# A planned issue order with new durations, due times and join rounds: an audio tower on one core

## The chip, the cores and the metric

The kernel runs on 1 core of one Trainium2 chip. The time is the device time of one execution in microseconds (us). Three runs before the change took 18586.4, 18587.15 and 18591.35 us; their median is 18587.15.

## What is computed

A batch of 32 signals is cut into S = 313 frames of 512 samples. A DCT, one attention layer and one feed-forward layer follow:

```python
h = einsum('bfh,kh->bfk', frames, D)                     # DCT
h = h + attention(layernorm(h))
h = h + ffn(layernorm(h))

# attention, 8 heads of 64
Q, K = xpos(X W_Q), xpos(X W_K); V = X W_V
p = softmax(Q K^T) * gamma^|i-j|
Y = groupnorm(p V)
return (silu(X W_G) * Y) W_O

# ffn: 256 units n, over 512 features d
theta = x[d] / (1 + |W[n,d]|) + B[n,d]
idx = round(theta * 4096/2pi) mod 4096
cos_sum[n] = sum_d cos(idx) * attn_cos[n,d]              # the same with sin
return silu(cos_sum proj_cos^T + sin_sum proj_sin^T)
```

Nearly all the work is in the feed-forward layer: 32 x 313 x 256 x 512 angles, each with a sine and a cosine.

## The kernel before, in words

**Feed-forward in rounds.** The 256 units are taken in 8 blocks of 32 (UNITS), and the sequences in pairs. A round (ffn_round, line 574) does one block for all pairs that are in the ring; a pair is in the ring for 8 rounds in a row, one for each block. STARTS (line 33) names the round in which each of the 16 pairs joins. A ring of one to four pairs means r = 2, 4, 6 or 8 sequences side by side. A slot holds 24 sequence-columns of S: 12 units of 2 sequences, 6 of 4, 4 of 6 or 3 of 8. For each slot VectorE (DVE) writes the indices as int16, one instruction per unit (line 612), adds a quarter turn for the cosine in a second tile (621), and masks both (628). ScalarE (ACT) makes two sine tiles of 128 x 7512 elements from them (line 636). TensorE (PE) sums each tile over features with one-hot weights, 24 products a tile (line 658), into PSUM banks pa; at the end of a round VectorE copies the sums out (675) and SP stores them. There are five index tiles (N_IX) and two sine tiles (N_TRIG): ACT cannot start the second tile after one that TensorE still reads. SP loads the block's one-hot weights (604), the factors f (592) and the normalised inputs xT (596).

**Attention in between.** Each sequence has to have gone through DCT, layer norm, attention and the second layer norm before its pair can join. The function attention (line 302) does this for one sequence in the buffers of A. Its stages: the product with the DCT by rows (line 282), a layer norm on VectorE (245 to 260) whose reciprocal root is a Newton iteration of 12 small steps on GpSimd (POOL, lines 233 to 236), transposes (269), values by rows, four times queries and keys by columns (297) with a rotary step on VectorE, scores (374) with maximum and subtraction on VectorE (382, 385), exponentials on ACT (400, or 404 where few pairs run), per head transposes (428), decay (440) and value products (446), the gate by columns, group norm with a second Newton chain (three columns times eight heads), output product by rows, second layer norm, and a store of xT to memory. The first two sequences run before the first sine, in two sets of buffers A and B. Output (line 528) multiplies a pair's finished sums by the projection and adds the residual.

**What sets the order.** Nothing is scheduled at run time: each engine runs its instructions in a fixed order. The class Plan collects operations with a key (when it is due), an engine, a duration in ns and what it reads and writes. Its emit walks through them with one clock for each engine: on the engine that is free first it issues, among what is ready by then, the operation with the lowest key. A result on another engine counts as ready 300 ns later (WAIT), a DMA 2500 ns after its issue (LAND). One unit of key is one full sine tile; key_of[rd] is the number of such tiles before round rd. The feed-forward's operations have the key of their tile. Attention of a sequence has a window of keys (times, lines 797 to 804, spread so that each pair is finished 8 tiles before it joins), and its stages' keys are spread over that window by step (line 309):

```python
def step(n=1.0):
    done[0] += n
    return keys(done[0] / 135.0)
```

where the stages together add up to 139. The durations are the third argument of plan.add, as 880 for a row product (line 281), 550 for a column product (296), 800 for three transposes (273, 432), 660 for scores (373), 1000 for three value products (452), 6000 for a Newton chain (239), 150 for each product of the sums (666).

Of the kernel before, what the change touches and what calls it, by code (L numbers as in the profile page):

```python
# [22 lines left out]
HOP = 512  # L23
# [2 lines left out]
LUT = 4096  # L26
NC4 = HOP // P
EPS = 1e-5
RING = 8
UNITS = 32  # L30
SLOT = 24

STARTS = (0, 4, 8, 10, 12, 14, 16, 18, 20, 22, 24, 26, 28, 30, 32, 34)
NT = 3


# [6 lines left out]
DMA_NS = 500.0  # L43
# [83 lines left out]
def tile_audio_tower(ctx: ExitStack, tc: tile.TileContext, t: dict, out: bass.AP):  # L127
    nc = tc.nc
    n_seq, S = t["frames"].shape[0], t["frames"].shape[3]
    STEP = (S - 1) // NT  # L130
    N = S - STEP * (NT - 1)
# [89 lines left out]
    def rsqrt(plan, key, val, r, u, kv, kr, ku):  # L221

        def seed():
            nc.vector.tensor_scalar(
                u.bitcast(I32), val.bitcast(I32), 1, None, ALU.logical_shift_right
            )
            nc.vector.tensor_scalar(  # L227
                r.bitcast(I32), u.bitcast(I32), -1.0, float(RSQRT_SEED), ALU.mult, ALU.add
            )

        def newton():
            for _ in range(3):
                nc.gpsimd.tensor_tensor(u, r, r, ALU.mult)  # L233
                nc.gpsimd.tensor_tensor(u, u, val, ALU.mult)
                nc.gpsimd.tensor_scalar(u, u, -0.5, 1.5, ALU.mult, ALU.add)
                nc.gpsimd.tensor_tensor(r, r, u, ALU.mult)

        plan.add(key, "DVE", 400, seed, (kv,), (kr, ku))
        plan.add(key, "POOL", 6000, newton, (kv,), (kr, ku))

    def layernorm(plan, key, x):

# [21 lines left out]
    def transposed(plan, key, x):  # L264

        for c in range(NC4):
            def go(c=c):
                for i in range(NT):
                    nc.tensor.transpose(
                        x.W[:, c, ROW0[i] : ROW0[i] + N], x.h[:N, i, c * P : (c + 1) * P],  # L270
                        ident[:N, :N],
                    )
            plan.add(key, "PE", 800, go, x.rows_of, x.banks(c))

    def rows(plan, key, x, lhsT, src, r, order=range(NT), src_r=()):

        for c in range(NC4):
            k = x.load(plan, key, src[c], src_r)
            for to, i in enumerate(order):
                plan.add(  # L280
                    key, "PE", 880,
                    lambda c=c, i=i, k=k, to=to: nc.tensor.matmul(  # L282
                        x.W[:N, to, :], lhsT[:, c, ROW0[i] : ROW0[i] + N], x.ring[k],
                        start=(c == 0), stop=(c == NC4 - 1)
                    ),
                    (*r, x.k("ring", k)), x.banks(to),
                )

    def columns(plan, key, x, bank, src):

        k = x.load(plan, key, src)

        w = x.ring[k].rearrange("p (c n) -> p c n", n=P)
        for c in range(NC4):
            plan.add(
                key, "PE", 550,
                lambda c=c: nc.tensor.matmul(x.W[:, bank, :S], w[:, c, :], x.xnT[:, c, :],  # L297
                                             start=(c == 0), stop=(c == NC4 - 1)),
                (x.k("xnT"), x.k("ring", k)), x.banks(bank),
            )  # L300

    def attention(plan, keys, sq, x, eng, swap_m=None):
# [3 lines left out]

        done = [0.0]

        def step(n=1.0):
            done[0] += n  # L310
            return keys(done[0] / 135.0)

        def residual(key, load):
            for i in range(NT):
# [5 lines left out]
                else:  # L320
# [2 lines left out]

        hs, probs, room, us = x.rows_of, x.probs, x.room, x.every("u", 2)
        W3 = x.W[:N, :NT, :]
        plan.add(step(0), "SP", DMA_NS, lambda: nc.sync.dma_start(x.u, t["frames"][sq]), (), us)
        rows(plan, step(7), x, x.u, t["dct"], us)
        copy(plan, step(), eng, NT * HOP, x.h[:N], W3, x.banks(0, 1, 2), hs)
        residual(step(0), False)
        layernorm(plan, step(3), x)  # L330
        transposed(plan, step(3), x)
        copy(plan, step(), eng, NC4 * S, x.xnT, x.W[:, :, :S], x.banks(0, 1, 2, 3), (x.k("xnT"),))


        rows(plan, step(7), x, x.xnT, wv_d, (x.k("xnT"),), range(NT - 1, -1, -1),
             ("wv_d",))
        copy(plan, step(), eng, NT * HOP, x.h[:N], W3, x.banks(0, 1, 2), hs)
        plan.add(step(0), "POOL", 500, lambda: nc.gpsimd.memset(x.h[0:1, : NT - 1, :], 0.0), (), hs)

        plan.add(step(0), "SP", DMA_NS, lambda: nc.sync.dma_start(x.table, t["turn_qk"]),  # L340
                 (), probs[-4:-2])

        def rotary(g):
            key = step(4)
            qk, kq = x.qk[g % 2], x.k("u", g % 2)
            columns(plan, key, x, 0, t["wq"][g])
            columns(plan, key, x, 1, t["wk"][g])

            if swap_m is None:
                columns(plan, key, x, 2, t["wq_s"][g])  # L350
                columns(plan, key, x, 3, t["wk_s"][g])
            else:
                copy(plan, key, eng, 2 * S, x.raw, x.W[:, 0:2, :S], x.banks(0, 1), probs[-1:])
                for i in range(2):
                    plan.add(key, "PE", 550,
                             lambda i=i: nc.tensor.matmul(x.W[:, 2 + i, :S], swap_m, x.raw[:, i, :],
                                                          start=True, stop=True),
                             probs[-1:], x.banks(2 + i))
            plan.add(key, "DVE", 1500,
                     lambda: nc.vector.tensor_tensor(x.turn, x.W[:, :, :S], x.table, ALU.mult),  # L360
                     (*probs[-4:-2], *x.banks(0, 1, 2, 3)), probs[-2:])
            plan.add(key, "DVE", 870,
                     lambda: nc.vector.tensor_tensor(
                         qk, x.turn[:, 0:2], x.turn[:, 2:4], ALU.add),
                     probs[-2:], (kq,))

        def scores(hd):
            key = step(2.5)
            r0 = (hd % 2) * DH
            qk, kq = x.qk[hd // 2 % 2], x.k("u", hd // 2 % 2)  # L370
            for i in range(NT):
                plan.add(
                    key, "PE", 660,
                    lambda i=i: nc.tensor.matmul(  # L374
                        x.W[:N, i, :S], qk[r0 : r0 + DH, 0, ROW0[i] : ROW0[i] + N],
                        qk[r0 : r0 + DH, 1, :], start=True, stop=True,
                    ),
                    (kq,), x.banks(i),
                )
# [17 lines left out]
        def exps():  # L397
# [3 lines left out]
            else:  # L401
                for a in range(H):
# [2 lines left out]
                                             accum_out=x.sm[:N, i, a : a + 1])  # L405

            nc.scalar.activation(x.lu[:1, 0:1], x.lu[:1, 0:1], AF.Silu)
        plan.add(step(2), "ACT", 18200 if eng == "ACT" else 9500, exps,
                 (), [*probs, x.k("sm"), x.k("lu")])
        if eng == "DVE":  # L410
            for a in range(0, H, 2):
                plan.add(step(0), "DVE", 2080,
                         lambda a=a: nc.vector.tensor_reduce(
                             x.sm[:N, :, a : a + 2].rearrange("p i h -> p h i"),
                             x.prob[:N, a : a + 2], AX.X, ALU.add),
                         probs[a : a + 2], (x.k("sm"),))
        for hd in range(H):
            key = step(5)
            a, d = hd, hd % 2
            plan.add(key, "SP", DMA_NS,  # L420
                     lambda hd=hd, d=d: nc.sync.dma_start(x.dec[d], t["decay"][hd]),
# [1 line left out]
            for jj in range(NT):  # L423
                j = NT - 1 - jj

                def go(a=a, jj=jj, j=j):
                    for i in range(NT):
# [1 line left out]
                            x.W[:N, jj, ROW0[i] : ROW0[i] + N],  # L429
                            x.prob[:N, a, i, ROW0[j] : ROW0[j] + N], ident[:N, :N],  # L430
                        )
                plan.add(key, "PE", 800, go, (probs[a],), x.banks(jj))

            def decayed(a=a, d=d):
                window = x.dec[d][:N].rearrange("p (a s) -> p a s", a=1)
# [7 lines left out]
            for i in range(NT):  # L443
                def go(i=i, hd=hd, a=a):
                    for jj in range(NT):
# [3 lines left out]
                            x.h[:N, jj, hd * DH : (hd + 1) * DH],  # L449
                            start=(jj == 0), stop=(jj == NT - 1),  # L450
                        )
                plan.add(key, "PE", 1000, go, (probs[a], hs[hd // 2]), x.banks(3))
            if hd % 2 == 0:
                continue


            h0 = hd - 1
            plan.add(
                step(), "DVE", 560,
                lambda h0=h0: nc.vector.tensor_copy(  # L460
                    x.h[:N, :, h0 * DH : (h0 + 2) * DH], x.y[:N]),
                x.banks(3), (hs[h0 // 2],),
            )


        key = step(6)
        for g in range(NC4):
            columns(plan, key, x, g, t["wg"][g])
        plan.add(step(), "ACT", 1270,
                 lambda: nc.scalar.activation(x.u, x.W[:, :, :S], AF.Silu),  # L470
                 x.banks(0, 1, 2, 3), us)


        xh = x.h[:N].rearrange("p i (h e) -> p (i h) e", e=DH)
        key = step(5)
        if eng == "ACT":
            plan.add(key, "ACT", 1500,
                     lambda: nc.scalar.activation(x.sq[:N], x.h[:N], AF.Square), hs, room)
# [22 lines left out]
                 (x.k("gr"),), hs)  # L501


        transposed(plan, step(4), x)
        residual(step(0), True)
        key = step(2)
        for c in range(NC4):
            plan.add(key, "DVE", 530,
                     lambda c=c: nc.vector.tensor_scalar(
# [2 lines left out]
                     x.banks(c), room)  # L512
        plan.add(key, "DVE", 1460,
                 lambda: nc.vector.tensor_tensor(x.u, x.u, x.aff, ALU.mult), room, us)
        rows(plan, step(7), x, x.u, t["wo"], us)
        plan.add(step(2), "DVE", 1760,
                 lambda: nc.vector.tensor_tensor(x.h[:N], x.h[:N], W3, ALU.add),
                 x.banks(0, 1, 2), hs)
        residual(step(0), False)
        layernorm(plan, step(3), x)  # L520
        transposed(plan, step(3), x)
        key = step()
        copy(plan, key, eng, NC4 * S, x.u, x.W[:, :, :S], x.banks(0, 1, 2, 3), us)
        plan.add(key, "SP", DMA_NS,
                 lambda: nc.sync.dma_start(xT_d[:, :, sq * S : (sq + 1) * S], x.u),
# [48 lines left out]
    def ffn_round(plan, k0, blk, ring):  # L574
# [9 lines left out]
        key = k0  # L584
        for parts in slots:
# [45 lines left out]
            for k in (1, 0):  # L631
# [13 lines left out]
                def go(k=k, w=w, parts=parts, first=first):  # L645
# [4 lines left out]
                    for nc2 in dict.fromkeys((n // 2, c) for n, c in parts):  # L650
                        for bk, p in enumerate(banks[k]):
                            alone = r - 4 * bk == 2
                            for pt, (n, c) in enumerate(parts):
                                u = n % 2
                                for b in range(min(4, r - 4 * bk) if (n // 2, c) == nc2 else 0):
# [7 lines left out]
                                        stop=(n - u == UNITS - 2 and c == NC4 - 1  # L663
                                              and (alone or u == 1)),
                                    )
                plan.add(key, "PE", 150 * len(parts) * r, go,
                         (("trig", w), *(("hot", hot[n // 4 * 4, c]) for n, c in parts)),
                         [("pa", p) for p in banks[k]])
                key += len(parts) * r / SLOT
# [270 lines left out]
```

## Time and profile before

| what | us |
|---|---|
| median of three runs | 18587.15 |
| the profiled execution | 18593.15 |
| its span, first to last instruction | 18591.2 |
| ScalarE busy (of it sine tiles, line 636) | 17827.2 (17398.1) |
| VectorE busy (indices 6499.2, quarter turns 2905.2, masks 5581.8) | 17165.7 |
| TensorE busy (sums, line 658: 10304.5) | 14520.5 |
| GpSimd busy | 968.9 |

The mean granted clock of TensorE is 0.918 of full speed. A group's "busy" is the time in which at least one of its instructions ran; consecutive sines overlap a little at their ends, so that one lasts 6.45 us from its start to its end and 6.36 from one start to the next. "Idle before" names what ended a wait. The profile can be cut into stretches of time; since rounds are told by counting sine tiles in ACT's order, each round has a place in time: round 0 begins at 316 us, round 4 (the second pair joins) at 1017, round 14 (the sixth pair) at 4555, round 34 (the last pair) at 15777.

### The profile page before, as it was taken

The numbers are of one execution on the slowest core, as the hardware profiler recorded it, in microseconds if no ns is written. First come the engines' busy times: TensorE is split into PE (matmuls) and PEld (weight loads), VectorE is DVE, ScalarE is ACT, GpSimd is POOL, SyncE is SP. The second block draws the span as 40 slices with busy tenths as digits, with TensorE's granted clock in tenths as the row PEclk, the third lists the DMA queues.
The fourth block names the chain that finished last, engine by engine and source line by source line (L and its number), as shares of the span: only waits on it lengthen the run. The fifth ranks groups of instructions, "written<-read, shape, count | busy, mean of one in ns | idle before, by whom it ended". The sixth has DMA issues, their size and how long they took to land. (4 is left out here: it accounts for less than half of the span.)

```text
span 18591.2 us, 325962 instructions
## 1 busy us (share of the span) xinstructions
PE 14520.5 (78%) x148768; PEld 6791.6 (37%) x148768; DVE 17165.7 (92%) x11210; ACT 17827.2 (96%) x3248; POOL 968.9 (5%) x1222
## 2 busy tenths in 40 slices
PE   8788888888777877778877787877788777666666
PEld 5443333334333333333333333333333333222222
DVE  6989999999999999999999999999999999888887
ACT  4899999999999999999999999999999999999998
POOL 0000000000000000000000000000000000000000
PEclk8899999999999999999999999999999999888888
DMA  3221121121111111111111111111111111001011
GB/s 94 71 66 56 60 67 58 54 61 58 45 38 47 57 50 52 45 45 57 48 58 47 43 53 48 58 48 55 39 50 57 48 56 42 29 21 33 20 40 53
DMA packets 598691, 942.55 MB, mean 51 GB/s; under 512 B 116768, under 2 KB 337952, under 8 KB 586048
## 3 DMA queue, kind: packets, MB, share of 16 engines
q1 hardware_dynamic: 597312, 921.70, 16.0%
q8 instruction: 1166, 19.10, 0.4%
q14 instruction: 213, 1.74, 0.0%
HBM read 816.78 MB, written 104.66 MB: 50 GB/s over the span
## 5 line engine op out<-in xcount | busy, mean ns | idle before, releaser
L636 ACT ACTIVATE trig<-ix 128x7512 f32<-128x7512 int16 (+1 forms) x2760 | 17398.1, 6386 | 456.8 <-PE pa L658 229.7
L658 PE MATMUL pa<-trig,hot 128*32 128x313 f32 x131072 | 10304.5, 468 | 3545.1 <-ACT trig L636 3530.3
L658 PEld LDWEIGHTS pa<-trig,hot 128*32 128x32 f32 x131072 | 4291.2, 118 | 9312.4 <-ACT trig L636 4578.4
L612 DVE TENSOR_SCALAR ix<-xT,f 128x2504 int16<-128x2504 f32 (+3 forms) x5376 | 6499.2, 1268 | 431.6 <-ACT trig L636 389.4
L628 DVE TENSOR_SCALAR ix<-ix 128x15024 int16<-128x15024 int16 (+4 forms) x1656 | 5581.8, 3385 | 41.1
L621 DVE TENSOR_SCALAR ix<-ix 128x7512 int16<-128x7512 int16 (+1 forms) x1380 | 2905.2, 2105 | 356.1 <-ACT trig L636 264.4
L297 PE MATMUL a_W<-a_xnT,a_ring 128*128 128x313 f32 x4896 | 1426.2, 437 | 40.9 <-DVE a_prob L385 15.4
L282 PE MATMUL a_W<-a_ring,a_u 128*105 128x512 f32 x2256 | 1087.5, 625 | 141.2 <-DMA a_u<-in_frames 52.9
L297 PEld LDWEIGHTS a_W<-a_xnT,a_ring 128*128 128x128 f32 x4896 | 891.8, 190 | 580.1 <-issue 212.5
L282 PEld LDWEIGHTS a_W<-a_ring,a_u 128*105 128x105 f32 x2256 | 374.7, 177 | 756.3 <-issue 615.0
L233 POOL TENSOR_TENSOR a_gu<-a_gr 105x24 f32<-105x24 f32 x93 | 104.5, 1124 | 9461.6 <-DVE a_gr L227 9456.7
L446 PE MATMUL a_W<-a_h,a_prob 105*105 105x64 f32 x4464 | 483.0, 264 | 77.6 <-DVE a_prob L440 77.4
L374 PE MATMUL a_W<-a_u 64*105 64x313 f32 x1488 | 477.7, 453 | 72.1 <-DVE a_prob L385 40.0
L446 PEld LDWEIGHTS a_W<-a_h,a_prob 105*105 105x105 f32 x4464 | 447.3, 177 | 212.1 <-issue 143.7
L282 PE MATMUL a_W<-a_ring,a_xnT 128*105 128x512 f32 x744 | 350.6, 611 | 22.3 <-DVE a_xnT L219 20.5
L233 POOL TENSOR_TENSOR a_lu<-a_lr 105x3 f32<-105x3 f32 x186 | 141.1, 759 | 4073.3 <-DVE a_lr L227 4063.6
L374 PEld LDWEIGHTS a_W<-a_u 64*105 64x105 f32 x1488 | 234.0, 171 | 310.8 <-DVE a_prob L385 79.2
L428 PE MATMUL a_W<-ident,a_prob 105*105 105x105 f32 x2232 | 284.9, 272 | 44.1 <-DVE a_h L460 26.1
L382 DVE TENSOR_REDUCE a_mx<-a_W 105x3 f32<-105x939 f32 x248 | 280.1, 1130 | 37.6 <-PE a_W L374 36.5
L428 PEld LDWEIGHTS a_W<-ident,a_prob 105*105 105x105 f32 x2232 | 237.9, 178 | 159.4 <-issue 92.5
L440 DVE TENSOR_TENSOR a_prob<-a_W,a_u 105x939 f32<-105x939 f32 x248 | 279.8, 1128 | 16.3 <-PE a_W L428 10.9
L385 DVE TENSOR_TENSOR a_prob<-a_W,a_mx 105x939 f32<-105x939 f32 x248 | 281.7, 1136 | 8.5
(134 smaller groups left out, 3386.8 us busy)
## 6 DMA issues: line engine op xcount, KB each, us to landing
hot<-in_hot SPq DMA_DIRECT2D x1344, 128.0 KB
xT<-xT_d SPq DMA_DIRECT2D x88, 1252.0 KB
a_u<-in_decay SPq DMA_DIRECT2D x248, 260.5 KB
a_ring<-in_proj SPq DMA_DIRECT2D x128, 256.0 KB
a_ring<-in_dct SPq DMA_DIRECT2D x124, 256.0 KB
a_ring<-wv_d SPq DMA_DIRECT2D x124, 256.0 KB
a_ring<-in_wq SPq DMA_DIRECT2D x124, 256.0 KB
a_ring<-in_wk SPq DMA_DIRECT2D x124, 256.0 KB
```

Of the source, the lines that this page charges most:

```text
L282: lambda c=c, i=i, k=k, to=to: nc.tensor.matmul(x.W[:N, to, :], lhsT[:, c, ROW0[i] : ROW0[i] + N], x.ring[k], start=(c == 0), stop=(c == N ...
L297: lambda c=c: nc.tensor.matmul(x.W[:, bank, :S], w[:, c, :], x.xnT[:, c, :], start=(c == 0), stop=(c == NC4 - 1)),
L374: lambda i=i: nc.tensor.matmul(x.W[:N, i, :S], qk[r0 : r0 + DH, 0, ROW0[i] : ROW0[i] + N], qk[r0 : r0 + DH, 1, :], start=True, stop=True,),
L382: lambda: nc.vector.tensor_reduce(m[:N], x.W[:N, :NT, :S], AX.X, ALU.max),
L385: lambda: nc.vector.tensor_tensor(x.prob[:N, hd], x.W[:N, :NT, :S], m[:N].unsqueeze(2).to_broadcast((N, NT, S)), ALU.subtract),
L428: nc.tensor.transpose(x.W[:N, jj, ROW0[i] : ROW0[i] + N], x.prob[:N, a, i, ROW0[j] : ROW0[j] + N], ident[:N, :N],)
L446: nc.tensor.matmul(x.y[:N, i, (hd % 2) * DH : (hd % 2 + 1) * DH], x.prob[:N, a, jj, ROW0[i] : ROW0[i] + N], x.h[:N, jj, hd * DH : (hd + 1) ...
L612: nc.vector.tensor_scalar(ix[:, x[0], pt * r * S : (pt + 1) * r * S], now["xT", y][:, : r * S], f[:, 0, n : n + 1], f[:, 1, n : n + 1], AL ...
L621: nc.vector.tensor_scalar(ix[:, x[1], :E], ix[:, x[0], :E], float(LUT // 4), None, ALU.add)
L628: nc.vector.tensor_scalar(ix[:, i, :E], ix[:, i, :E], LUT - 1, LUT // 2, ALU.bitwise_and, ALU.bitwise_xor)
L636: nc.scalar.activation(tl[:, :E], ix[:, x[1 - k], :E], AF.Sin, bias=-PI32, scale=ANG)
L658: nc.tensor.matmul(now["pa", p][g * 32 : g * 32 + 32, :S], now["hot", hot[n // 4 * 4, c]][:, n % 4, k, :], now["trig", w][:, s0 : s0 + S], ...
```

## The change: what it does

- STARTS: pairs 2, 3, 4 and on join in rounds 7, 9, 11, ... rather than 8, 10, 12, ..., and the last two in 32 and 35 rather than 32 and 34 (numbers of pairs count from 0). There are 43 rounds instead of 42.
- step takes the name of a stage, and each stage moves the due time by its share: SHARE over their sum, WHOLE = 142.5. The last stage is due at the end of the window, not at 139/135 of it.
- The durations of TensorE's groups and of the Newton chain in the plan are others.
- The sums of a tile get a key that is lower by one tile.

```diff
+SHARE = dict(rows=5.0, copy=2.5, norm=8.0, turn=0.7, rotary=4.2, scores=3.2, exps=2.0, head=3.5,
+             pair=0.8, gate=4.1, silu=1.0, group=10.7, affine=5.5)
+TIMES = dict(rows=3, copy=5, norm=2, turn=3, rotary=4, scores=8, exps=1, head=8, pair=4, gate=1,
+             silu=1, group=1, affine=1)
+WHOLE = sum(SHARE[k] * TIMES[k] for k in SHARE)
...
-STARTS = (0, 4, 8, 10, 12, 14, 16, 18, 20, 22, 24, 26, 28, 30, 32, 34)
+STARTS = (0, 4, 7, 9, 11, 13, 15, 17, 19, 21, 23, 25, 27, 29, 32, 35)
...
-        plan.add(key, "POOL", 6000, newton, (kv,), (kr, ku))
+        plan.add(key, "POOL", 7500, newton, (kv,), (kr, ku))
...
-            plan.add(key, "PE", 800, go, x.rows_of, x.banks(c))
+            plan.add(key, "PE", 400, go, x.rows_of, x.banks(c))
...
-                    key, "PE", 880,
+                    key, "PE", 970,
...
-                key, "PE", 550,
+                key, "PE", 600,
...
-        def step(n=1.0):
-            done[0] += n
-            return keys(done[0] / 135.0)
+        def step(stage=None):
+
+            if stage:
+                done[0] += SHARE[stage]
+            return keys(done[0] / WHOLE)
...
-        rows(plan, step(7), x, x.u, t["dct"], us)
-        copy(plan, step(), eng, NT * HOP, x.h[:N], W3, x.banks(0, 1, 2), hs)
-        residual(step(0), False)
-        layernorm(plan, step(3), x)
-        transposed(plan, step(3), x)
+        rows(plan, step("rows"), x, x.u, t["dct"], us)
+        copy(plan, step("copy"), eng, NT * HOP, x.h[:N], W3, x.banks(0, 1, 2), hs)
+        residual(step(), False)
+        layernorm(plan, step("norm"), x)
+        transposed(plan, step("turn"), x)
...
-            key = step(4)
+            key = step("rotary")
...
-                    plan.add(key, "PE", 550,
+                    plan.add(key, "PE", 600,
...
-            key = step(2.5)
+            key = step("scores")
...
-                    key, "PE", 660,
+                    key, "PE", 640,
...
-            key = step(5)
+            key = step("head")
...
-                plan.add(key, "PE", 800, go, (probs[a],), x.banks(jj))
+                plan.add(key, "PE", 400, go, (probs[a],), x.banks(jj))
...
-                plan.add(key, "PE", 1000, go, (probs[a], hs[hd // 2]), x.banks(3))
+                plan.add(key, "PE", 680, go, (probs[a], hs[hd // 2]), x.banks(3))
...
-        key = step(6)
+        key = step("gate")
...
-        key = step(5)
+        key = step("group")
...
-        key = step(2)
+        key = step("affine")
...
-                plan.add(key, "PE", 150 * len(parts) * r, go,
+                plan.add(key - 1, "PE", 150 * len(parts) * r, go,
```

The other calls of step change in the same way: each takes the name of its stage where it took a number, and nothing where it took 0.

More of the change, by code (lines that the diff above doesn't have):

```diff
@@ L325, in attention @@
         W3 = x.W[:N, :NT, :]
-        plan.add(step(0), "SP", DMA_NS, lambda: nc.sync.dma_start(x.u, t["frames"][sq]), (), us)
-        rows(plan, step(7), x, x.u, t["dct"], us)
-        copy(plan, step(), eng, NT * HOP, x.h[:N], W3, x.banks(0, 1, 2), hs)
-        residual(step(0), False)
-        layernorm(plan, step(3), x)
-        transposed(plan, step(3), x)
-        copy(plan, step(), eng, NC4 * S, x.xnT, x.W[:, :, :S], x.banks(0, 1, 2, 3), (x.k("xnT"),))
-        rows(plan, step(7), x, x.xnT, wv_d, (x.k("xnT"),), range(NT - 1, -1, -1),
+        plan.add(step(), "SP", DMA_NS, lambda: nc.sync.dma_start(x.u, t["frames"][sq]), (), us)
+        rows(plan, step("rows"), x, x.u, t["dct"], us)
[3 more added lines that the diff above has]
+        transposed(plan, step("turn"), x)
+        copy(plan, step("copy"), eng, NC4 * S, x.xnT, x.W[:, :, :S], x.banks(0, 1, 2, 3), (x.k("xnT"),))
+        rows(plan, step("rows"), x, x.xnT, wv_d, (x.k("xnT"),), range(NT - 1, -1, -1),
              ("wv_d",))
-        copy(plan, step(), eng, NT * HOP, x.h[:N], W3, x.banks(0, 1, 2), hs)
-        plan.add(step(0), "POOL", 500, lambda: nc.gpsimd.memset(x.h[0:1, : NT - 1, :], 0.0), (), hs)
-        plan.add(step(0), "SP", DMA_NS, lambda: nc.sync.dma_start(x.table, t["turn_qk"]),
+        copy(plan, step("copy"), eng, NT * HOP, x.h[:N], W3, x.banks(0, 1, 2), hs)
+        plan.add(step(), "POOL", 500, lambda: nc.gpsimd.memset(x.h[0:1, : NT - 1, :], 0.0), (), hs)
+        plan.add(step(), "SP", DMA_NS, lambda: nc.sync.dma_start(x.table, t["turn_qk"]),
                  (), probs[-4:-2])
         def rotary(g):
-            key = step(4)
+            key = step("rotary")
             qk, kq = x.qk[g % 2], x.k("u", g % 2)
@@ L407, in exps @@
             nc.scalar.activation(x.lu[:1, 0:1], x.lu[:1, 0:1], AF.Silu)
-        plan.add(step(2), "ACT", 18200 if eng == "ACT" else 9500, exps,
+        plan.add(step("exps"), "ACT", 18200 if eng == "ACT" else 9500, exps,
                  (), [*probs, x.k("sm"), x.k("lu")])
@@ L411, in attention @@
             for a in range(0, H, 2):
-                plan.add(step(0), "DVE", 2080,
+                plan.add(step(), "DVE", 2080,
                          lambda a=a: nc.vector.tensor_reduce(
@@ L458, in attention @@
             plan.add(
-                step(), "DVE", 560,
+                step("pair"), "DVE", 560,
                 lambda h0=h0: nc.vector.tensor_copy(
@@ L463, in attention @@
             )
-        key = step(6)
+        key = step("gate")
         for g in range(NC4):
             columns(plan, key, x, g, t["wg"][g])
-        plan.add(step(), "ACT", 1270,
+        plan.add(step("silu"), "ACT", 1270,
                  lambda: nc.scalar.activation(x.u, x.W[:, :, :S], AF.Silu),
@@ L501, in attention @@
                  (x.k("gr"),), hs)
-        transposed(plan, step(4), x)
-        residual(step(0), True)
-        key = step(2)
+        transposed(plan, step("turn"), x)
+        residual(step(), True)
+        key = step("affine")
         for c in range(NC4):
@@ L514, in attention @@
                  lambda: nc.vector.tensor_tensor(x.u, x.u, x.aff, ALU.mult), room, us)
-        rows(plan, step(7), x, x.u, t["wo"], us)
-        plan.add(step(2), "DVE", 1760,
+        rows(plan, step("rows"), x, x.u, t["wo"], us)
+        plan.add(step("copy"), "DVE", 1760,
                  lambda: nc.vector.tensor_tensor(x.h[:N], x.h[:N], W3, ALU.add),
                  x.banks(0, 1, 2), hs)
[L519 to L522, printed above, removed]
+        residual(step(), False)
+        layernorm(plan, step("norm"), x)
+        transposed(plan, step("turn"), x)
+        key = step("copy")
         copy(plan, key, eng, NC4 * S, x.u, x.W[:, :, :S], x.banks(0, 1, 2, 3), us)
```

## The prediction

> **What bounds the kernel now.** I read the engines' busy shares first, then the table of busy time by stretch, then who ScalarE (ACT) waited for, then the timeline at two waits.
>
> ```profile
> span 18591.2 us, 325962 instructions
> ...
> PE 14520.5 (78%) x148768; PEld 6791.6 (37%) x148768; DVE 17165.7 (92%) x11210; ACT 17827.2 (96%) x3248; POOL 968.9 (5%) x1222
> ```
>
> ACT computes the 2760 sine tiles and is busy for all but 764 us of the span. An issue order can give back only those 764 us. The stretches below are cut where rounds 0, 4, 10, 14, 18, 34 and 38 begin on ACT (found by counting sine tiles); the columns are length, then busy time of PE, PEld, DVE, ACT, POOL.
>
> ```profile
> 0.00:316.00 316.00, 265.07 (x992) 171.67 (x992) 144.74 (x178) 51.42 (x124) 19.96 (x82) 0.79 0.35 107
> 316.00:1017.00 701.00, 562.86 (x5149) 287.30 (x5150) 641.92 (x759) 587.98 (x201) 44.68 (x76) 0.89 0.25 74
> 1017.00:2808.00 1791.00, 1457.16 (x14464) 704.33 (x14467) 1722.64 (x1406) 1689.60 (x342) 114.11 (x155) 0.93 0.20 62
> 2808.00:4555.00 1747.00, 1436.21 (x14432) 695.72 (x14436) 1684.67 (x1136) 1675.63 (x282) 123.62 (x150) 0.93 0.19 57
> 4555.00:6823.00 2268.00, 1794.43 (x18590) 837.75 (x18581) 2115.66 (x1249) 2217.52 (x370) 133.92 (x164) 0.92 0.15 47
> 6823.00:15777.00 8954.00, 7149.66 (x74399) 3346.19 (x74399) 8476.63 (x4961) 8874.92 (x1489) 532.63 (x596) 0.93 0.16 50
> 15777.00:17694.00 1917.00, 1258.84 (x14416) 509.71 (x14416) 1632.47 (x870) 1905.82 (x305) 0.00 (x0) 0.88 0.08 26
> 17694.00:18591.20 897.20, 596.27 (x6336) 238.96 (x6336) 746.94 (x659) 824.31 (x139) 0.00 (x0) 0.87 0.16 47
> ```
>
> Length less ACT's busy time gives its idle time: 265 us before the first sine, 113 + 101 + 71 = 286 in rounds 0 to 13, 50 + 79 = 130 in rounds 14 to 33, 11 + 73 = 84 at the end (44 of them the last output's matrix product). Rounds 0 to 13 belong to VectorE: it is busy 4049 of 4239 us, 96 more than ACT's 3953, and its own idle time is 190; 96 + 190 is just ACT's 286. A stall of ACT that is removed there pays nothing unless VectorE's work or idle time shrinks. From round 18 VectorE has slack, and ACT's waits count one for one:
>
> ```profile
> ACT trig L636 <- PE pa L658: 58.2, 44, 8.8
> ACT trig L636 <- issue: 48.5, 13, 6.5
> ACT trig L636 <- DVE ix L628: 12.8, 8, 3.2
> ```
>
> (Waits of ACT in rounds 14 to 33: us, times, longest.) The 58 us are attention's matrix products that stand between the sums of two tiles. Those put to "issue" are mostly of one kind, seen once per pair in the timeline: the first DCT products wait for the frames' DMA (issued at 9011.98, product at 9018.60) and the ready sums stand behind them.
>
> **The change, part by part.**
>
> *Rounds.* Every sum of ACT's work stays: 2758 sine tiles in place of 2760, of the same elements. VectorE's index instructions change form, since a wider ring does the same elements in fewer instructions. From the rows by form (busy over count) one costs 0.527 us for 2 sequences, 0.861 for 4, 1.196 for 6, 1.525 for 8. Over the run there are 128 more of the first, 128 fewer of the second, 384 more of the third, 256 fewer of the fourth: 67 - 110 + 459 - 390 = +26 us, and four more copies of sums (0.48 each), +28. But where they fall counts. Pair 5 joins at sine tile 608 before and 606 after; until then two rounds of two pairs are replaced by one of four: 128 x 1.525 - 256 x 0.861 = **-25 us** of VectorE's work in the stretch that it bounds, -26 with two copies fewer. The +54 elsewhere come after the last joins, where rounds 34 to 37 show 285 us of VectorE idle, so nothing. If that cover were gone they would cost at most 54. One more round has a single pair, and three rather than two have two: by the waits of rounds 38 to 40 (4 to 9 us of ACT idle in each), +8. The 32 more one-hot loads, 4 more loads of f and 32 more stores of sums go through SP and DMA queues that are 8 to 35% busy: nothing. The last pair joins at tile 2411 instead of 2304 (in full tiles of work); this thins attention in the last third, where ACT waits little already: nothing.
>
> *Newton steps due after 7.5 us instead of 6.* Rows of the POOL chain give 8.9 us (median, three columns) and 10.7 us (24 columns), and VectorE waits for it 54 us in rounds 0 to 13, 28 waits. Taken at its word the edit saves up to 1.5 us of each, 42. But the timeline shows what makes the chain long:
>
> ```profile
> 8987.09 4.56 DVE L612 TENSOR_SCALAR ix<-xT,f 128x2504 int16<-128x2504 f32 x3
> ...
> 8988.80 1.42 POOL L234 TENSOR_TENSOR a_lu<-a_lu,a_lv 105x3 f32<-105x3 f32 x1
> ...
> 8991.80 2.14 POOL L236 TENSOR_TENSOR a_lr<-a_lr,a_lu 105x3 f32<-105x3 f32 x1
> ...
> 8994.01 0.19 POOL L233 TENSOR_TENSOR a_lu<-a_lr 105x3 f32<-105x3 f32 x1
> ...
> 8996.19 1.46 DVE L257 TENSOR_SCALAR a_h<-a_h,a_mv,a_lr 105x512 f32<-105x512 f32 x3 [2.31 <-POOL a_lr L236]
> ```
>
> While VectorE runs index instructions, POOL gets one step done per VectorE instruction (1.4 to 4 us); when VectorE stops, the eight left take 0.28 each, which is the wait of 2.31. 1.5 us more of index work in front lets one or two more steps through, 0.3 to 0.6 us a wait: 28 waits give **-10** (ends: 0 and -42).
>
> The Trainium skill's page "SBUF — State Buffer", section on who interferes with whom, says the same more sharply: VectorE and GpSimd share a port pair, and whichever holds it blocks the other for a whole instruction. By that rule the edit would save next to nothing and the sum below end 10 us later; by the planner's arithmetic it would save the 42.
>
> *TensorE's durations and sums first.* Trace per planned group: three transposes 0.38 us (planned 0.8, now 0.4), three value products 0.65 (1.0, now 0.68), a row product 0.96 (0.88, 0.97), a column product 0.58 (0.55, 0.60), scores 0.64 (0.66, 0.64). With the key of a sum lowered by one tile, attention waits when both are ready. A tile lasts 6.36 us on ACT and its sums 3.37, so over 3 us of attention between two sums delays ACT. In the two issue orders, at these durations, such gaps fall from 81 to 26 among tiles 1300 to 2100 (37 to 14 among 600 to 950): row products go three per tile, not in runs of six. A third of 58 us leaves 19, **-39**; ends 0 and -58. The DMA waits stay, each perhaps a row product shorter (13 x 0.6): **-6**, ends 0 and -48. In the first 460 tiles such gaps rise from 133 to 153, but VectorE bounds there.
>
> What this uncovers: the old plan's too long transposes and value products were a cushion. Sums take 3.77 us on average (10304.5 over 2731 full tiles) and 5.06 where TensorE had idled just before, and the plan still has 3.6. Attention's results can now arrive after VectorE's place for them in its fixed order, and the index work behind waits too. VectorE waits for TensorE for some 33 us in rounds 0 to 13. I take half as much again, **+15**; ends -33 (all go) and +100 (a third of about 200 hand-overs, 20 a sequence in rotary, scores and heads, late by 5.06 - 3.6). After round 14 VectorE's idle time (25 to 40 us a round) covers it.
>
> *Stages due by share.* The last stage was due at 139/135 of a sequence's window and is now due at its end. At the join of round 4 VectorE waited 19.4 us for xT, and ACT 13.4. Three per cent of some 300 us are 9; VectorE is full there, so I take **-5** (0 to -19). Before the first sine both sequences keep their order but for two heads and some loads: 0, ends -10 and +10.
>
> **Sum.** -26 + 8 - 10 - 39 - 6 + 15 - 5 = -63. The profiled execution took 18593.15 us (span 18591.2), 6 above the median of the runs, 18587.15: forecast 18530 for such a run, **18525** for the median.
>
> **Rivals.** *More (0.17):* the truer plan halves VectorE's 190 us of early idle time, and the middle's 107 us go: -26 - 95 - 90 + 8, 18385 at the far end and 18450 midway to the forecast. For: every duration moved is nearer its row. Against: 73 of the 190 us are POOL's chain and xT's DMA.
> *Nothing (0.20):* the early gain is lost to late attention and the middle's stalls only move, as the frames' DMA stays; -10, -5 and +8 are left: 18580. For: tighter joins for pairs 2 to 4 (43, 21 and 21 tiles earlier) ask for attention sooner, and VectorE's excess over ACT peaks at 93 us in the new order against 95 in the old, by summing both engines' instructions in order. Against: the counts above.
> *Slower (0.13):* VectorE waits on TensorE in rounds 0 to 12, the cushion gone and sums ahead. At 1.46 us each it passes the gain when 53 more hand-overs are late (78 / 1.46); with 100 late, +146 - 78 = +68: 18655.
> *Forecast (0.50).*
>
> **How the numbers follow.** 0.2% is about what a measurement of this kernel can tell from no change: below 18550 is faster, over 18624 slower. Of the forecast's 0.5 some 0.45 lie below 18550: faster 0.62, same 0.25, slower 0.13. The range 18430 to 18625 takes in the unknown ends of the middle and the cushion and leaves the slow rival and the far end out.
>
> **What would show it.** ACT's waits for TensorE in the middle near 20 us; the DMA kind still once a pair; VectorE's waits for POOL still over 1 us each; ACT's idle time until pair 5 joins near 260; a tail some 8 longer. Wrong if VectorE's idle time until pair 5's join is over 250 us, or if sums stall ACT elsewhere.

## The result, and the profile after

The changed kernel takes 18460.92 us (median; 18458.81 to 18468.71), the one before 18588.39 on the same chip: ratio 0.9932, 95% interval 0.9921 to 0.9944, so 127.5 us faster. The range held it; the forecast of 18525 had half of the gain.

The page's span and busy line, and the busy time by stretch. The cuts are the starts of rounds 0, 4 (pair 1 joins), 9, 13 (pair 5 joins: the counterpart of 4555 us before), 17, 35 (the last pair joins: the counterpart of 15777) and 37; columns as before.

```profile
span 18457.0 us, 326424 instructions
...
PE 14446.5 (78%) x148768; PEld 6739.2 (37%) x148768; DVE 17189.2 (93%) x11340; ACT 17817.8 (97%) x3246; POOL 1128.9 (6%) x1222
```

```profile
0.00:327.00 327.00, 261.49 (x992) 168.66 (x992) 145.43 (x180) 51.52 (x125) 19.99 (x82) 0.79 0.36 103
327.00:1019.00 692.00, 555.83 (x5153) 284.54 (x5154) 641.72 (x758) 588.28 (x202) 46.58 (x76) 0.90 0.26 75
1019.00:2663.00 1644.00, 1358.74 (x13408) 663.00 (x13406) 1589.45 (x1243) 1552.42 (x317) 141.56 (x152) 0.93 0.21 61
2663.00:4516.00 1853.00, 1520.17 (x15452) 727.51 (x15452) 1789.09 (x1163) 1809.90 (x304) 159.18 (x152) 0.93 0.19 55
4516.00:6746.00 2230.00, 1783.72 (x18609) 831.27 (x18607) 2123.55 (x1254) 2216.93 (x373) 157.18 (x158) 0.94 0.17 49
6746.00:16343.00 9597.00, 7577.23 (x79560) 3502.27 (x79560) 9073.91 (x5345) 9550.70 (x1596) 604.38 (x603) 0.93 0.16 49
16343.00:17166.00 823.00, 541.16 (x6196) 219.43 (x6200) 709.11 (x413) 817.50 (x132) 0.00 (x0) 0.88 0.10 29
17166.00:18457.00 1291.00, 848.15 (x9408) 342.48 (x9400) 1116.95 (x992) 1230.54 (x204) 0.00 (x0) 0.88 0.15 43
```

ACT's work is what it was (17817.8 busy, 9 less); its idle time fell from 764 to 639 us. Until pair 5 joins VectorE's work fell from 4049 to 4020 us (641.72 + 1589.45 + 1789.09), its idle time from 190 to 169, and ACT's idle time from 286 to 238. POOL, which has the same 1222 instructions, is busy 160 us longer. ACT's waits from there to the last join (us, times, longest; "issue" where the profile shows nothing that ended the wait):

```profile
ACT trig L644 <- PE pa L666: 25.3, 11, 4.3
ACT trig L644 <- issue: 24.7, 10, 3.8
```

These two were 58.2 and 48.5, and the wait for VectorE, 12.8, is gone. "The middle" below is this stretch.

### The profile page after: what moved, and what is told of

The parts are those of the page before. It is cut to its first block, busy times and chain, and to the rows that moved or that the text cites. A ratio compares the mean times of both kernels' runs of the same rounds, so it can differ in the third digit from the quotient of the medians.

```text
span 18457.0 us, 326424 instructions
## 1 busy us (share of the span) xinstructions
PE 14446.5 (78%) x148768; PEld 6739.2 (37%) x148768; DVE 17189.2 (93%) x11340; ACT 17817.8 (97%) x3246; POOL 1128.9 (6%) x1222
## 3 DMA queue, kind: packets, MB, share of 16 engines
q1 hardware_dynamic: 604032, 926.03, 16.9%
## 5 line engine op out<-in xcount | busy, mean ns | idle before, releaser
L239 POOL TENSOR_TENSOR a_lu<-a_lr 105x3 f32<-105x3 f32 x186 | 197.8, 1063 | 4617.1 <-DVE a_lr L233 4528.9
L288 PE MATMUL a_W<-a_ring,a_xnT 128*105 128x512 f32 x744 | 355.0, 614 | 10.1 <-ACT a_xnT L223 5.4
```

Of the source, the lines that this page charges most:

```text
L288: lambda c=c, i=i, k=k, to=to: nc.tensor.matmul(x.W[:N, to, :], lhsT[:, c, ROW0[i] : ROW0[i] + N], x.ring[k], start=(c == 0), stop=(c == N ...
```

## The experiments

Five parts can be undone or done by themselves: the join rounds, the due times by share, the sums' key, TensorE's durations, the Newton chain's duration. Each kernel's time is compared with runs of the kernel before on the same chip. The gains below are its median less that of before; an interval is 16 to 25 us wide to each side, so differences of 10 to 15 between two kernels are not clear of noise. Of each kernel one execution was profiled.

| kernel | gain, us | ratio (95%) | ACT idle before first sine | rounds 0-3 | to pair 5 | to pair 13 | rest |
|---|---|---|---|---|---|---|---|
| before | | | 265 | 113 | 173 | 113 | 100 |
| changed, all five | 127 | 0.9932 (0.9921-0.9944) | 275 | 104 | 135 | 53 | 72 |
| old rounds | 90 | 0.9950 (0.9936-0.9963) | 276 | 105 | 169 | 44 | 94 |
| old due times | 79 | 0.9957 (0.9945-0.9970) | 277 | 106 | 152 | 74 | 86 |
| sums not first | 141 | 0.9924 (0.9912-0.9937) | 276 | 88 | 138 | 53 | 67 |
| old TensorE durations | 115 | 0.9937 (0.9925-0.9950) | 270 | 128 | 155 | 32 | 70 |
| old Newton duration | 117 | 0.9938 (0.9925-0.9950) | 275 | 93 | 141 | 72 | 78 |
| rounds alone | 55 | 0.9973 (0.9962-0.9984) | 262 | 116 | 163 | 94 | 75 |
| due times alone | 6 | 0.9997 (0.9989-1.0006) | 262 | 128 | 173 | 98 | 98 |
| sums first alone | -6 | 1.0004 (0.9995-1.0012) | 265 | 127 | 175 | 111 | 98 |
| TensorE durations alone | 5 | 1.0000 (0.9991-1.0009) | 275 | 99 | 165 | 108 | 106 |
| rounds and due times | 43 | 0.9979 (0.9970-0.9988) | 263 | 127 | 166 | 96 | 73 |
| due times and Newton | 21 | 0.9990 (0.9981-0.9999) | 270 | 133 | 193 | 70 | 86 |
| sums not first, frames late | 104 | 0.9944 (0.9932-0.9957) | 272 | 107 | 156 | 57 | 72 |

The idle times are from each kernel's profile, which lies within 11 us of its median, cut by counting sine tiles where pairs 1, 5 and 13 join.

What stood in front of the sums when ACT waited for them is not told by the labels of the waits: the same kind of wait appears under "PE pa" and under "issue". One such wait of the changed kernel:

```profile
8922.14 0.42 SPq L334 DMA_DIRECT2D a_u<-in_frames  x1
...
8928.99 4.49 PE L288 MATMUL a_W<-a_ring,a_u 128*105 128x512 f32 x6 [4.69 <-DMA a_u<-in_frames]
...
8933.41 3.37 PE L666 MATMUL pa<-trig,hot 128*32 128x313 f32 x48
...
8936.90 6.47 ACT L644 ACTIVATE trig<-ix 128x7512 f32<-128x7512 int16 x1 [3.33 <-PE pa L666]
```

The first DCT product waits for the frames' load, the sums stand behind it, and ACT is 3.33 us late, under "PE pa". The next table puts both labels together. To each wait of ACT from pair 5's join to the last it assigns the attention product that waited longest on TensorE in the 14 us before, if one waited over 1 us (us, times; with 10 us in place of 14 the first row of before is 35.8 and the last 34.4).

| behind | before | changed | old due times | old Newton | due times alone | sums not first | the same, frames late |
|---|---|---|---|---|---|---|---|
| the first DCT product | 42.2 (9) | 26.7 (9) | 34.2 (8) | 41.2 (10) | 52.7 (9) | 25.9 (9) | 16.9 (8) |
| transposes after a norm | 18.3 (10) | 14.2 (6) | 9.6 (5) | 10.1 (6) | 13.8 (8) | 18.0 (9) | 11.3 (8) |
| another product | 19.5 (10) | 0 | 3.0 (2) | 11.8 (5) | 18.8 (8) | 0 | 19.1 (12) |
| no product that waited | 26.7 (28) | 9.2 (6) | 24.9 (15) | 12.5 (13) | 23.8 (30) | 7.3 (10) | 11.6 (11) |

### One part undone

**Rounds.** The changed kernel with the old STARTS.

```diff
-STARTS = (0, 4, 7, 9, 11, 13, 15, 17, 19, 21, 23, 25, 27, 29, 32, 35)
+STARTS = (0, 4, 8, 10, 12, 14, 16, 18, 20, 22, 24, 26, 28, 30, 32, 34)
```

> The changed kernel with the old join rounds (0, 4, 8, 10, ..., 34). Theory (each part pays in its own stretch: the rounds by 26 us less of VectorE's work until pair 5 joins, TensorE's planned durations by ACT's waits in the middle and at the end): 18485 to 18510 us, with ACT's waits for TensorE in the middle still near 25 us, and VectorE busy some 27 us less over the run. Rival (the rounds carry nearly all, because the stretch that VectorE bounds ends earlier): 18550 or more. Rival (the rounds are neutral): 18455 to 18465.

18500.19 us: 37 of the gain go, as my theory had it. In the profile, which is 11 us above the median, ACT idles 35 us more until pair 5 joins and 22 more after pair 13, and 9 less between. VectorE's work until pair 5 joins is back at 4049 us.

**Due times.** The changed kernel with step(n) and its numbers over 135 again.

```diff
-            if stage:
-                done[0] += SHARE[stage]
-            return keys(done[0] / WHOLE)
+            done[0] += n
+            return keys(done[0] / 135.0)
```

> The changed kernel with the old stage steps (numbers over 135). Theory (due times matter little, as VectorE is full early and has slack later): 18460 to 18480 us. Rival (the spread of VectorE's attention over each window is what frees ACT): 18520 or more, with VectorE as the one that ACT waits for.

18511.17 us: 48 of the gain go, against my 0 to 20. The time lies between the two ranges, nearer the rival's, but VectorE is not what ACT waits for most. Who ACT waits for after pair 5:

```profile
ACT trig L636 <- issue: 45.0, 14, 6.2
ACT trig L636 <- PE pa L658: 26.6, 16, 5.4
ACT trig L636 <- DVE ix L628: 14.3, 8, 4.4
```

The wait for VectorE, none in the changed kernel, is back, but it is the smallest of the three. The two others come to 72 us against 50. Behind the first DCT product 8 us more are lost than in the changed kernel, and 16 more where no product had waited: no one kind of wait carries it.

**Sums first.** The key is the tile's own again.

```diff
-                plan.add(key - 1, "PE", 150 * len(parts) * r, go,
+                plan.add(key, "PE", 150 * len(parts) * r, go,
```

> The changed kernel with the sums' key at their own tile again. In its issue order 38 gaps between two sums among tiles 1300 to 2100 hold over 3 us of attention, against 26 changed and 81 before. Theory (the durations do most of it): 18465 to 18485 us. Rival (sums first is what took ACT's waits for TensorE away): 18500 or more.

18449.72 us, below both ranges: 13 more gained than with it. ACT's waits in the middle are unchanged (25.2 for TensorE and 26.0 put to "issue"); rounds 0 to 3 lose 16 us of idle time. The edit that seemed made for ACT's waits did nothing for them, and the best kernel of the study is the one without it; its interval overlaps the changed one's, so that "harmless to leave out" is shown, "harmful" is not.

**TensorE's durations.**

```diff
-            plan.add(key, "PE", 400, go, x.rows_of, x.banks(c))
+            plan.add(key, "PE", 800, go, x.rows_of, x.banks(c))
...
-                    key, "PE", 970,
+                    key, "PE", 880,
```

and likewise 600 to 550, 640 to 660, 680 to 1000.

> The changed kernel with TensorE's old planned durations (800, 880, 550, 660, 1000). 76 of the gaps among tiles 1300 to 2100 hold over 3 us of attention, near the 81 of before. Theory (these durations carry the gain in the middle and at the end): ACT's waits for TensorE in the middle back near 55 us, those at the end near 20: 18500 to 18530 us. Rival (sums first and due times carry it): 18455 to 18475.

18475.97 us, at the upper edge of the rival's range: 13 go, which is not clear of noise. In the profile the loss is all before pair 5 joins (rounds 0 to 3 idle 24 us more, up to pair 5 20 more, before the first sine 6 less). In the middle it is the other way round. ACT's waits from pair 5's join to the last:

```profile
ACT trig L644 <- PE pa L666: 22.1, 18, 5.0
ACT trig L644 <- issue: 9.2, 5, 3.1
```

31 us, less than the 50 of the changed kernel, though this order has 76 gaps with over 3 us of attention among tiles 1300 to 2100 where the changed one has 26. My count of such gaps does not foretell these waits.

**Newton chain.** 7500 back to 6000.

> The changed kernel with the Newton chain planned at 6000 again. Theory (VectorE's index work holds POOL up, so a later due time lengthens the chain and saves only 0.3 to 0.6 us a wait): 18465 to 18480 us. Rival (this is what lets the due times work: together they gain some 60 us that neither has alone): 18490 to 18520.

18473.58 us: 10 of the gain go, the size I had, though 10 is not clear of noise. The place is not the one I had. Up to pair 5 it changes nothing (93 + 141 against 104 + 135); in the middle VectorE waits 109 us for POOL instead of 65 between pair 5 and pair 13, and up to the last join ACT waits 76 us behind TensorE instead of 50, 41 of them behind the first DCT product instead of 27:

```profile
ACT trig L644 <- PE pa L666: 50.7, 24, 6.1
ACT trig L644 <- issue: 24.8, 10, 4.2
```

### One part, or two, alone

**The rounds alone** (the STARTS lines above, put into the kernel before).

> The kernel before with the new join rounds alone. Undone alone they cost 39 us. Theory (they are worth the same by themselves, since VectorE's work until pair 5 joins falls by 26 us and nothing else depends on it): 18540 to 18565 us, ACT's waits for TensorE in the middle still near 52. Rival (they pay only together with the new due times): 18575 to 18600.

18535.63 us, 55 gained: more than I expected, and the only part that pays alone. VectorE's work until pair 5 joins falls as worked out (4025 against 4049 us), but its idle time there rises from 190 to 205, and ACT's idle time falls by only 7. The rest of the gain is up to pair 13 (19) and after it (25); ACT's waits for TensorE between pair 5 and pair 13 are 36 us, not near 52.

**The due times alone** (SHARE, WHOLE and step of the change in the kernel before).

> The kernel before with the stages due by share alone. Undone alone this cost 50 us, which the prediction had put at 5. Theory (it spreads attention, and acts by itself in rounds 0 to 13 and in the middle): 18530 to 18550 us, with fewer of ACT's DMA-bound waits in the middle (25 instead of 41) . Rival (it pays only with true durations): 18570 or more.

18584.8, in the rival's range: nothing that can be told from no change. What undoing them costs is therefore not theirs alone. The expected sign did not come either: behind the first DCT product ACT waits 53 us, more than before.

**Sums first alone.**

> The kernel before with the sums' key lower by one tile alone. Undone alone it gained 11 us, all before round 4 and at the end. Theory (it only helps where attention is badly placed otherwise, so on the old plan it takes ACT's waits for TensorE in the middle from 52 towards 20, though rounds 0 to 3 lose): 18550 to 18580 us. Rival (it does harm everywhere or nothing): 18590 to 18610.

18595.81: nothing, and 14 us more idle time in rounds 0 to 3, about as much as undoing it saved there. The rival was right.

**TensorE's durations alone.**

> The kernel before with TensorE's new durations alone. Undone alone they cost 15 us, all before pair 5 joins; in the middle their absence cost nothing. Theory (any one of due times, sums first and durations takes ACT's waits for TensorE in the middle away, so that taking back one shows nothing): 18540 to 18565 us, with those waits near 20. Rival (the durations matter only early): 18570 to 18590, with those waits near 50.

18585.27: nothing in sum. Of 14 us saved in rounds 0 to 3, 10 are paid before the first sine, and ACT's waits for TensorE between pair 5 and pair 13 are 66, not near 20. So they do not remove these waits by themselves, and the idea that any one of three parts does so falls.

**Rounds and due times together.**

> The kernel before with the new join rounds and the new due times, all durations and the sums' key old. Alone the rounds gained 55 us and the due times 6. Theory (the due times fit the new rounds, in which VectorE's bound ends earlier; durations add little): 18470 to 18490 us. Rival (the due times need true durations too): 18520 to 18535, the two parts' plain sum.

18547.78: 43 gained, not more than the rounds alone. Both ranges were off; what the due times are worth in the changed kernel needs the changed durations or keys as well.

**Due times and the Newton chain, old rounds.**

> The kernel before with the new due times and the Newton chain at 7500, old rounds. Theory (the two do not depend on each other): 18570 to 18585 us. Rival (the due times need the later Newton chain): 18540 to 18560.

18569.47: 21 gained, at the lower edge of the theory's range. With due times alone ACT idles 98 us between pair 5 and pair 13, with the Newton chain added 70. There VectorE waits 50 us for POOL, against 90 with the due times alone and 87 in the changed kernel with the old due times, which has the Newton chain at 7500: there the two work together. Up to pair 5 this kernel is worse (326 us idle in rounds 0 to 13 against 301).

### A kernel that was to be better

The changed kernel without sums first, and with the frames' load planned to land later. The plan's add takes a landing time of its own for it:

```diff
-    def add(self, key, eng, dur, fn, r=(), w=()):
-        self.ops.append((key, eng, dur, fn, tuple(r), tuple(w)))
+    def add(self, key, eng, dur, fn, r=(), w=(), land=LAND):
+        self.land.append(land)
+        self.ops.append((key, eng, dur, fn, tuple(r), tuple(w)))
...
-            end = t + dur + (self.LAND if e == "SP" else 0.0)
+            end = t + dur + (self.land[i] if e == "SP" else 0.0)
```

and 6000.0 as the last argument of the frames' load.

> The changed kernel without sums first, and with the frames' load planned to land 6000 ns after its issue rather than 2500 (in the trace of before the first product came 6.6 us after the issue). Without sums first alone it took 18450. Theory (ready sums stand behind the first DCT product, which waits for this load): the 25 us of ACT's waits of that kind in the middle go, 18415 to 18435 us. Rival (the load is late since SP issues it late, or another product takes its place): 18445 to 18455.

18486.22 us, 36 more than without the landing time, so the rival's range is off as well, but the second of its reasons shows. Where ACT waits less behind the first DCT product (16.9 us against 25.9), another product takes its place (19.1 against none). The first DCT product itself still waits for the frames, 24.0 us in 11 waits in the middle, against 23.4 in 12 without the landing time; why it did not move was not traced. The idle time up to pair 13 stays (57 us against 53). One such place in the timeline, gaps in brackets:

```profile
9014.84 1.45 DVE L226 COPY a_xnT<-a_W 128x1252 f32<-128x1252 f32 x1
...
9016.35 4.52 PE L289 MATMUL a_W<-a_ring,a_xnT 128*105 128x512 f32 x6 [2.68 <-DVE a_xnT L226]
...
9020.80 6.53 PE L668 MATMUL pa<-trig,hot 128*32 128x313 f32 x96
...
9024.29 6.46 ACT L646 ACTIVATE trig<-ix 128x7512 f32<-128x7512 int16 x1 [3.84 <-PE pa L668]
```

The value products stand in TensorE's order ahead of two tiles of sums and wait for VectorE's copy; the sums run together when they are through, and ACT is 3.84 us late. Most of the loss, 19 us in rounds 0 to 3 and 18 up to pair 5, I did not trace.

## Why the prediction was right or wrong, by its steps

**What bounds the kernel: right.** VectorE until pair 5 joins, ACT's waits after it. The idle time until pair 5 joins was put near 260; it is 238. Of the 58.2 us of ACT's waits for TensorE, which I had read as attention's own work between the sums, only 26.7 come without a product that had waited; 31.5 stand behind one that had.

**Rounds, -26: the work was sized rightly, the gain was mostly elsewhere.** VectorE's work until pair 5 joins fell by 29 us in the changed kernel and by 24 with the rounds alone, of which 25 were worked out from the forms. By themselves the rounds gain 55. Early they give 7; about 45 come after pair 5, the stretches that the step "nothing" and the +8 had covered. Up to pair 13 that gain is not the rounds' own: undone in the changed kernel, they leave ACT 9 us less idle there.

**The tail, +8: wrong in sign.** I had put ACT's 4 to 9 us of idle time in rounds 38 to 40 to the rounds themselves. Counted by round in the changed kernel, round 41 has one pair and idles 0.1 us, round 40 has one pair and the output of a pair that just ended, and idles 6.6; rounds 37 to 39 idle 1.6 to 2.4 each. After the round of the last join 77 us became 63. This points to outputs rather than to narrow rounds, but it was not tested, and before the change round 39 idles 8.6 with two pairs and no pair just ended.

**Newton, -10: right on the chain, by luck on the time.** POOL's chain, measured from its first to its last step, grew from 8.9 to 12.6 us (median, three columns) and from 10.7 to 13.2; POOL's 160 us of added busy time are this. VectorE's waits for it until pair 5 joins fell from 54 to 45. The timeline of the changed kernel, like the lines of before at a sequence's second layer norm:

```profile
8899.48 2.12 DVE L629 TENSOR_SCALAR ix<-ix 128x7512 int16<-128x7512 int16 x1
...
8901.63 4.14 DVE L636 TENSOR_SCALAR ix<-ix 128x7512 int16<-128x7512 int16 x2
...
8903.88 1.95 POOL L240 TENSOR_TENSOR a_lu<-a_lu,a_lv 105x3 f32<-105x3 f32 x1
...
8905.91 0.20 POOL L241 TENSOR_SCALAR a_lu<-a_lu 105x3 f32<-105x3 f32 x1
...
8907.53 1.46 DVE L263 TENSOR_SCALAR a_h<-a_h,a_mv,a_lr 105x512 f32<-105x512 f32 x3 [1.75 <-POOL a_lr L242]
```

The two masks of a slot, 4.14 us, now stand in front of the normalisation. POOL gets one step through beside each, then six are left, and VectorE still waits 1.75 us instead of 2.31. The Trainium skill's page "SBUF — State Buffer", section "Who interferes with whom", says that VectorE and GpSimd share a port pair, and that in VectorE's 2-port modes whichever has it blocks the other for a whole instruction. The trace agrees with it: 1.95 us for a step beside a mask, 0.20 without. Which mode the masks run in, no run here shows.

With 6000 put back VectorE's waits for POOL until pair 5 joins are 52, so some 7 to 9 us of them are saved, as forecast. But no time comes of it there: ACT idles 234 us until pair 5 joins with 6000 and 238 with 7500. What undoing costs falls after that. What the step did not have is that a Newton chain that is late can stall ACT through TensorE: in the middle ACT waits 76 us behind TensorE with 6000 and 50 with 7500. In the changed kernel four waits of ACT, of 2.0 to 2.1 us each, stand behind transposes that waited some 5 us for the group norm's multiplication, which waits for POOL.

**TensorE's durations and sums first, -39 - 6 + 15: the total fell about as said, the terms did not.** 58.2 and 48.5 us became 25.3 and 24.7: 33 less where 39 were forecast, and 24 where 6 were. By kinds, waits without a product that had waited, which the -39 was about, fell by 18, those behind the first DCT product by 16, still once a pair as said, and those behind norms and other products by 24. And the step that names the cause failed: sums first has no part in it (undone, the waits stay), the durations alone leave them, and a kernel with three times as many crowded gaps waits less. The cushion's price was put at +15. VectorE's waits for TensorE until pair 5 joins were 36 us (some 33 in the prediction) and rose by 7, but with the old durations put back they are 59, and the early stretches are worse by 44. The old durations were no cushion there. Before the first sine the new ones cost 10, within the ends given.

**Due times, -5: the step that failed.** xT's wait at the join of round 4 fell from 19.4 to 10.2 us, but not by the due times: it is 7.0 with them undone, and 11.4 with TensorE's durations alone. Undoing the due times costs 48 (in the profiles 19 us of idle time until pair 5 joins and 35 later). I took the spread of attention over its window to be free wherever an engine has slack. It is not: from pair 5's join to the last, ACT waits 72 us behind TensorE and 14 for VectorE with the old steps, 50 and none with the new ones. By themselves the due times leave 109 us behind TensorE, as before (107).

What they need beside them can be told for one wait. Between pair 5 and pair 13 VectorE waits 50 to 65 us for POOL in the six kernels that have both the new due times and the Newton chain at 7500, and 87 to 109 in the eight that lack one of the two or both. ACT idles there 32 to 70 us in the six, and 72 to 113 in the eight. How a later Newton chain and the due times make the wait shorter only together was not traced.

**The sum.** Rounds 55, due times 6, sums first -6, durations 5: 60 us by themselves, and some 10 to 15 for the Newton chain (117 against 127 from one side, 21 against 6 from the other). The changed kernel gains 127. Some 55 us belong to no single part; the small terms are not clear of noise, but these 55 are more than any one interval. Rounds and due times alone gain 43, and adding any two of durations, sums first and the Newton chain brings it to 115 or more (115, 117 and 141). Adding up parts, as the forecast did, had to miss this.

**The rivals.** 18461 lies 64 us below the forecast and 11 above the 18450 that the rival "more" (0.17) puts halfway to the forecast (18455 by its ends). Of its two causes one came by half: the middle's 107 us went down to 50. The other hardly came: VectorE's early idle time went from 190 to 169 us and was not halved. That the range held the time is the work of its wide ends, not of the sum.

**What stays open.** Which of those three the due times need for the whole of the gain: rounds and due times with just one of them were not run, nor the Newton chain alone. Why the rounds alone leave 19 us less idle time up to pair 13, where the rings are the same, was not traced.

## What to carry to other kernels

In an order that is fixed ahead, look for the instruction that waits in front of ready work, and ask what made the plan put it there. The label of a wait names what ended it; what stood in front has to be read from the timeline. Here parts of the planner's model paid together, and one at a time most showed nothing, so judge such a change by undoing parts of the whole as well as by adding them. The count of crowded gaps in the order did not foretell the waits; price them from a profile.

## What the runs showed of the hardware that was not expected

A step of 3 columns on GpSimd takes 0.2 us by itself and up to 4.0 beside a mask of VectorE (128x15024, 4.07 us). So a chain of 12 such steps has no duration that a plan could hold. Planned at 6000 ns it has a median of 8.8 to 8.9 us in the kernels here, planned at 7500 one of 12.3 to 12.6: 1.5 us more in the plan made it some 3.7 us longer. The shortest took 3.2.
